# Convolution rounds with one head at full width, and another order of their horizontal distances

## The chip, the cores and the metric

The kernel runs on one core of a Trainium2 chip. The metric is the device time of one execution in microseconds (us), lower being better. A core has a matrix engine (TensorE, "PE" in the profile, its weight loads "PEld"), a vector engine (DVE), a scalar engine (ACT), GpSimd (POOL) and a sync engine (SP) that issues most of the transfers. Each engine works through its own queue in the order in which the program was written, and waits on semaphores.

## The reference, cut to what matters

Two layers work on 4 images of 512 channels, 64 x 64 pixels, all in fp32. The change is in the first layer, a linear attention with two sets of heads. The second set is made from a 5 x 5 convolution, channel by channel, of queries, keys and values, followed by a mix of 8 channels within each head:

```python
qkv = jnp.moveaxis(jnp.concatenate([q, k, v], axis=-1), -1, 1)
dw = lax.conv_general_dilated(qkv, dw_kernel, (1, 1), 'SAME', feature_group_count=3 * INNER, dimension_numbers=DN)
pw = lax.conv_general_dilated(dw, pw_kernel, (1, 1), 'VALID', feature_group_count=3 * NUM_HEADS, dimension_numbers=DN)
qkv_all = jnp.concatenate([qkv, pw], axis=1)
...
scores = jnp.einsum('bhdn,bhen->bhde', value_pad, key_)
out = jnp.einsum('bhde,bhen->bhdn', scores, query)
out = out[:, :, :-1] / (out[:, :, -1:] + EPS)
...
y = lax.conv_general_dilated(out, proj_kernel, (1, 1), 'VALID', dimension_numbers=DN)
```

'SAME' means that pixels outside the image count as zero. The second layer takes edge maps of the result, multiplies them with four weight matrices, applies gelu, weighs channels, fuses them and normalizes.

## The kernel before

**Tiling.** The 512 channels are cut into 4 groups of 128 (16 heads of 8 channels), so there are 16 pairs of image and group, each a `Group` object. An image is cut into 8 strips of 512 pixels: strip j holds every fourth row of one half of the image (`STRIPS`, L48). `project` (L256) multiplies a strip with the key or query weights of the group, four matmuls of 128 x 128 by 128 x 512 accumulated in one bank of PSUM. ACT copies the bank to an SBUF tile `s` (L268), for queries also a rectified copy (L273), and issues four DMAs (L277) that lay the strip out again for the convolution: head set n of four goes to `inps[t][:, n]`, with partitions that hold rows modulo 4 and channels, and `NB` = 17 blocks of 4 rows by `W` = 64 columns in the free dimension. One such DMA moves 64 KB to 32 partitions, for each of them 8 blocks of 64 contiguous numbers. The first and the last block of `inps` are zeros, put there once by GpSimd (L142, L143), for the rows above and below the image.

**The convolution.** `convolve` (L388) does one half of the image, for keys or queries, with matrices that hold the products of both convolutions for 4 rows and 8 channels at a time. The matrix engine is used as sixteen pieces of 32 x 32: quarter i of the partitions by head j. The result has 8 blocks of rows by 64 columns, 512 pixels, for each of 16 pieces, in four banks (`quad_tiles`, L110). Ten rounds are accumulated: five horizontal distances dx (`DXS`, L53) times two blocks b of input rows. Each round issues sixteen matmuls, j outside and i inside, so that the first is i = j = 0. A distance other than 0 reaches over the edge of the image, where the input would be zero. So the columns c0 to c1 that are read and added to are shortened (`_span`, L78): 64 columns for dx = 0 (512 pixels), 63 for 1 and -1 (504 pixels), 62 for 2 and -2 (496 pixels). The first two rounds, dx = 0, write all 512 pixels. There are 64 convolutions in the kernel: 4 images x 4 groups x keys and queries x 2 halves. ACT then takes the banks out with a rectification (L409, L415).

**Order of the work.** The order on the matrix engine is the order of the program text. Lists written out by hand in `keys_and_values` (L557) and `queries` (L587) say in which order projections (`project`, `values`), transposes (`turn`, `conv_turn`), score products (`scores`, `correlate`) and convolutions of a group follow; the keys' convolutions come in the group's own `queries`, the queries' ones in the next group's `keys_and_values`. From the second image on, the stages of the image before (`project_out`, `edge_branches`, `fuse_out`) are woven in: each listed step has an estimated time (T_CONV is 10.6), and `advance` (L881) lets as many pieces of the other stages follow as are due. The last image's stages come at the end.

**DMA queues.** SP issues loads, the values' stores for the correlation (L297, 66 KB in runs of 264 bytes) and most others. ACT's queue issues the four DMAs of a projection and the edge branches' stores (L742)[...].

Of the kernel before, what the change touches and what calls it, by code (L numbers as in the profile page):

```python
# [8 lines left out]
F32 = mybir.dt.float32  # L9
# [4 lines left out]
B, C, H, W = 4, 512, 64, 64  # L14
N = H * W
P = 128
# [30 lines left out]
NB = H // 4 + 1  # L47
# [2 lines left out]

KV_ORDER = (1, 0, 2, 3, 4, 5, 6, 7)
Q_ORDER = (6, 7, 5, 4, 3, 2, 1, 0)
DXS = (0, -2, -1, 1, 2)  # L53
VROW = 4 * 66


# [21 lines left out]
def _span(d, n):  # L78

    return max(0, -d), n - max(0, d)  # L80
# [3 lines left out]
def conv_seq_kernel(  # L84
    ctx: ExitStack, tc, x, wqkv, dpk, wtab, proj, projc, pwk, bn0, consts, vec, watt1, batt1, watt2, wbr, wfuse, out
):
    nc = tc.nc
# [7 lines left out]
    keep = front.enter_context(tc.tile_pool(name="keep", bufs=1))  # L95
# [7 lines left out]
    def work_tile(name, n=512):  # L103
        return work.tile([P, 512], F32, tag="w", name=name)[:, :n]

    def ps_tile(name):
        return psum.tile([P, 512], F32, tag="ps", name=name)

    def quad_tiles(name):
        return [psum.tile([P, 512], F32, tag="quad", name=name) for _ in range(4)]  # L110

    def squares(ap):

        return ap.rearrange("p (b x n) -> p n x b", b=4, n=4)

    def rows(ap, width=W):
        return ap.rearrange("p (r c) -> p r c", c=width)
# [20 lines left out]

    inps = {}
    for t in (KEY, QUERY):  # L140
        inps[t] = keep.tile([P, 4, NB, W], F32, name=f"inp{t}")
        nc.gpsimd.memset(inps[t][:, :, 0, :], 0.0)  # L142
        nc.gpsimd.memset(inps[t][:, :, NB - 1, :], 0.0)  # L143

    vts = []
    for n in range(3):
# [73 lines left out]
    class Group:  # L220
# [35 lines left out]
        def project(self, t, j):  # L256
            half, k = STRIPS[j]
            if (self.b, j) not in xs:
                self.load_x(j)
            ps = ps_tile("proj")  # L260
            for c in range(NCH):
                nc.tensor.matmul(  # L262
                    ps, lhsT=self.w[t][:, c, :], rhs=xs[self.b, j][c], start=(c == 0), stop=(c == NCH - 1)
                )
            if t == QUERY and (self.g == NG - 1 or self.b and j not in KV_ORDER[:2]):
                del xs[self.b, j]
            s = work_tile("strip")
            nc.scalar.copy(s, ps)  # L268

            r, b = (k + 2) % 4, 8 * half + (k + 2) // 4  # L270
            if t == QUERY:
                self.rq[j] = work_tile("rq")
                nc.scalar.activation(self.rq[j], ps, AF.Relu)  # L273
            else:
                self.strip[j] = s
            for n in range(4):
                nc.scalar.dma_start(out=inps[t][r::4, n, b : b + 8, :], in_=rows(s)[32 * n : 32 * n + 32, :, :])  # L277

        def values(self, j):
            half, k = STRIPS[j]  # L280
# [106 lines left out]

        def convolve(self, t, half):  # L388
            banks = quad_tiles("cv")
            last = len(DXS) * 2 - 1  # L390
            for n, (dx, b) in enumerate((dx, b) for dx in DXS for b in range(2)):
                c0, c1 = _span(dx, W)
                for j in range(4):
                    for i in range(4):
                        q = slice(32 * i, 32 * i + 32)
                        nc.tensor.matmul(  # L396
                            rows(banks[i])[32 * j : 32 * j + 32, :, c0:c1],
                            lhsT=self.mat[t][q, j, (dx + 2) * 8 + 4 * b : (dx + 2) * 8 + 4 * b + 4, :],
                            rhs=inps[t][q, j, 8 * half + b : 8 * half + b + 8, c0 + dx : c1 + dx],
                            start=(n == 0), stop=(n == last),  # L400
                        )
            outs = []
            for i in range(4):
                o = work_tile("co")
                if t == KEY:
                    if half == 0 and i == 0:
                        self.ksum = mini.tile([P, 4, 4], F32, name="ksum")
                    for a in range(2):
                        nc.scalar.activation(  # L409
                            o.rearrange("p (n a x b) -> p a n x b", n=4, a=2, b=4)[:, a],  # L410
                            squares(banks[i][:, 256 * a : 256 * a + 256]), AF.Relu,
                            accum_out=self.ksum[:, 2 * half + a, i : i + 1],
                        )
                else:
                    nc.scalar.activation(o, banks[i], AF.Relu)  # L415
                outs.append(o)
            self.conv[t] = outs
# [494 lines left out]
    for n, cur in enumerate(groups):  # L912
# [5 lines left out]
        if n and n % NG == 0:  # L918
            last = groups[n - 1]
# [8 lines left out]
    last = groups[-1]  # L928
# [123 lines left out]
```

## Time and profile before

| | |
|---|---|
| median of 3 runs | 5082.15 us (5077.47 to 5088.09) |
| the profiled execution | 5063.71 us, with a span of 5061.9 us |
| PE busy | 4702.0 us, 93% |
| DVE, ACT, POOL busy | 2124.7, 1626.5, 392.7 us |
| projections of keys and queries, L262 | 955.8 us of PE in 2048 records |
| output projection, L655 | 899.6 us in 2048 records |
| convolution, L396 | 730.2 us in 20480 records |
| edge branches, L730 | 495.0 us in 2048 records |
| DMA bytes | 866.26 MB, 171 GB/s in the mean |
| granted clock of PE | 0.967 |

In the profile a line of a group names the source line, the engine, the operation, what is written and read, the shape and the count; after the bar stand busy time in us, the mean length of one in ns, and the idle time of the engine just before, with what ended it. Lengths of matmuls are modelled ends of pipelined work and overlap, above all for the sixteen pieces that run side by side, so their sum is not a time. A line of the timeline has the start in us, the length of the merged stretch in us, the engine and the count. A line of the waits has the waiting engine and line, what it waited for, and the total in us, the number of times and the longest. A line of a source has the operation, the count, and the shortest, median and longest length in ns. "issue" marks idle time in which an engine waited for nothing that the profile shows.

### The profile page before, as it was taken

Reading aid. Unit: us, or ns where it says so; the run is one execution under the profiler, and the core shown is the slowest. Engines: PE = TensorE matmul, PEld = TensorE weight load, DVE = VectorE, ACT = ScalarE, POOL = GpSimd, SP = SyncE. Lnnn points to the kernel's source line nnn. Section 1 sums busy time; section 2 is a strip of 40 time slices with the busy share of each in tenths; the row PEclk is TensorE's granted clock in tenths of the full one; section 3 lists DMA queues with packets and bytes.
Section 4 is the critical chain, followed back from the end, with each engine's and each line's share of the span. In section 5 each row is a group of like instructions: output and inputs, shape, how many; then the busy total and the mean of one; then the engine's idle time right before and its main releaser. Section 6 shows DMA issues by size and latency. Waiting matters only on the chain. (4 is left out here: it accounts for less than half of the span.)

```text
span 5061.9 us, 107134 instructions
## 1 busy us (share of the span) xinstructions
PE 4702.0 (93%) x46362; PEld 2739.7 (54%) x46362; DVE 2124.7 (42%) x2960; ACT 1626.5 (32%) x2833; POOL 392.7 (8%) x291
## 2 busy tenths in 40 slices
PE   9999999999999999799899999899989898898777
PEld 5665654455666554454465655454456665445443
DVE  1222221116556433211455653431146557157965
ACT  2112111004444423200345442320024445035765
POOL 0000000000000013100000000310000000001335
PEclk9999999999999999899999999999999999999889
DMA  6444466666656565676555665657655553774425
GB/s 196 138 123 130 132 206 190 158 165 181 192 189 183 179 205 170 197 178 156 176 176 181 193 202 176 213 188 167 163 173 175 184 169 129 200 184 118 151 88 172
DMA packets 635945, 866.26 MB, mean 171 GB/s; under 512 B 324393, under 2 KB 395081, under 8 KB 617041
## 3 DMA queue, kind: packets, MB, share of 16 engines
q1 hardware_dynamic: 551504, 758.68, 51.8%
q10 hardware_dynamic: 83968, 100.74, 6.4%
q8 instruction: 364, 5.96, 0.5%
q14 instruction: 109, 0.88, 0.1%
HBM read 578.09 MB, written 213.98 MB: 156 GB/s over the span
## 5 line engine op out<-in xcount | busy, mean ns | idle before, releaser
L262 PE MATMUL proj<-xt,w_sb 128*128 128x512 f32 x2048 | 955.8, 610 | 52.9 <-DMA xt<-in_x 31.8
L655 PE MATMUL yps<-hd,fold_sb 128*128 128x512 f32 x2048 | 899.6, 596 | 9.7 <-DMA hd<-heads 8.7
L396 PE MATMUL cv<-inp,mat 32*32 32x512 f32 x20480 | 730.2, 597 | 35.4 <-issue 27.3
L262 PEld LDWEIGHTS proj<-xt,w_sb 128*128 128x128 f32 x2048 | 382.7, 194 | 523.3 <-issue 450.7
L655 PEld LDWEIGHTS yps<-hd,fold_sb 128*128 128x128 f32 x2048 | 384.9, 190 | 493.5 <-issue 445.3
L396 PEld LDWEIGHTS cv<-inp,mat 32*32 32x32 f32 x20480 | 420.3, 103 | 314.6 <-issue 154.2
L730 PE MATMUL br<-maps,wbr_sb 128*128 128x256 f32 x2048 | 495.0, 396 | 51.8 <-ACT maps L713 42.2
L808 PE MATMUL zps<-ef,wf_sb 128*128 128x512 f32 x1024 | 469.9, 610 | 53.5 <-DMA ef<-ef 19.0
L730 PEld LDWEIGHTS br<-maps,wbr_sb 128*128 128x128 f32 x2048 | 399.7, 198 | 165.9 <-issue 51.3
L284 PEld LDWEIGHTS val<-w_sb,xt 128*128 128x128 f32 x4096 | 470.2, 192 | 33.9 <-issue 26.1
L284 PE MATMUL val<-w_sb,xt 128*128 128x128 f32 x4096 | 484.9, 277 | 0.6 <-DVE vt L291 0.3
L660 DVE SCALAR_TENSOR_TENSOR yt<-yps,shift,xr 128x512 f32<-128x512 f32 x128 | 96.1, 750 | 871.8 <-PE yps L655 788.9
L268 ACT COPY strip<-proj 128x512 f32<-128x512 f32 x256 | 149.1, 582 | 928.5 <-PE proj L262 910.4
L451 PE MATMUL corr<-near,ckt 128*32 128x160 f32 x8192 | 333.6, 315 | 35.0 <-DMA near<-near 28.4
L808 PEld LDWEIGHTS zps<-ef,wf_sb 128*128 128x128 f32 x1024 | 196.1, 195 | 296.6 <-issue 235.6
L241 POOL TENSOR_TENSOR mat<-dp_sb 128x1280 f32<-128x1280 f32 x32 | 77.2, 2414 | 3464.5 <-PE cv L396 2951.0
L451 PEld LDWEIGHTS corr<-near,ckt 128*32 128x32 f32 x8192 | 256.9, 111 | 131.5 <-issue 73.1
L703 DVE TENSOR_TENSOR maps<-dv 128x1054 f32<-128x1054 f32 x128 | 162.6, 1271 | 366.9 <-PE br L730 366.9
L312 ACT ACTIVATE kt<-tr 128x512 f32<-128x512 f32 x128 | 75.8, 593 | 528.9 <-PE tr L310 345.9
L737 ACT ACTIVATE ef_o<-br,shift,scale 128x256 f32<-128x256 f32 x256 | 142.3, 559 | 283.5 <-PE br L730 251.9
L360 DVE RECIPROCAL rec<-rec 128x512 f32<-128x512 f32 x64 | 214.4, 3350 | 1.7
L812 DVE TENSOR_SCALAR z<-zps,fbias 128x512 f32<-128x512 f32 x128 | 94.9, 744 | 283.4 <-DMA out<-z 97.0
(125 smaller groups left out, 4135.7 us busy)
## 6 DMA issues: line engine op xcount, KB each, us to landing
xt<-in_x SPq DMA_DIRECT2D x316, 512.0 KB
near<-near SPq DMA_DIRECT2D x512, 264.0 KB
inp<-strip ACTq DMA_DIRECT2D x1024, 64.0 KB
win<-y SPq DMA_DIRECT2D x128, 396.0 KB
near<-vt SPq DMA_DIRECT2D x512, 66.0 KB
y<-yt SPq DMA_DIRECT2D x128, 264.0 KB
yr<-y SPq DMA_DIRECT2D x128, 264.0 KB
heads<-q SPq DMA_DIRECT2D x128, 256.0 KB
```

What stands on the lines that cost most here:

```text
L262: nc.tensor.matmul(ps, lhsT=self.w[t][:, c, :], rhs=xs[self.b, j][c], start=(c == 0), stop=(c == NCH - 1))
L268: nc.scalar.copy(s, ps)
L284: nc.tensor.matmul(ps[:, ts(c, P)], lhsT=xs[self.b, j][n][:, ts(c, P)], rhs=self.w[VALUE][:, n, :], start=(n == 0), stop=(n == NCH - 1),)
L360: nc.vector.reciprocal(rec, rec)
L396: nc.tensor.matmul(rows(banks[i])[32 * j : 32 * j + 32, :, c0:c1], lhsT=self.mat[t][q, j, (dx + 2) * 8 + 4 * b : (dx + 2) * 8 + 4 * b + 4, :],
L451: nc.tensor.matmul(self.banks[jj][32 * i : 32 * i + 32, 160 * b : 160 * b + 160], lhsT=self.held["c", i][:, at : at + 32], rhs=v[:, 4 * n ...
L655: nc.tensor.matmul(ps, lhsT=fold_sb[g // NG][:, g % NG, ts(c, P)], rhs=hd[g], start=(g == 0), stop=(g == 2 * NG - 1),)
L660: nc.vector.scalar_tensor_tensor(yt[:, :, 1 : W + 1], rows(ps), shift0[:, c : c + 1], rows(xr), ALU.add, ALU.add)
L703: nc.vector.tensor_sub(flat[:, half : 3 * half - 2], dvs[:, 2 : 2 * half], dvs[:, 0 : 2 * half - 2])
L730: nc.tensor.matmul(rows(ps)[:, 4 * n : 4 * n + 4, :], lhsT=wbr_sb[:, k, c, :], rhs=rows(maps[c // 2][:, slot[k], c % 2, :], WB)[:, :, 0:W] ...
L737: nc.scalar.activation(o[:, n, :], ps[:, 256 * n : 256 * n + 256], AF.Gelu, bias=shift1[:, k : k + 1], scale=scale1[:, k : k + 1], accum_o ...
L808: nc.tensor.matmul(ps, lhsT=wf_sb[:, k, ts(c, P)], rhs=ef[k], start=(k == 0), stop=(k == 3))
```

## The change

The head set n = 0 (j = 0 in `convolve`) gets an SBUF tile of its own, with 68 columns: two zeros on each side of the 64. GpSimd clears the whole tile once. The other three keep their layout in a tile of three. In each round the first matmul, i = j = 0, reads all 64 columns from its tile, shifted by the distance, and adds to all 512 pixels; the zeros of the border stand for the pixels outside the image. The other fifteen matmuls keep their shortened spans; those of j = 0 with i = 1, 2, 3 read the bordered tile with a shortened span. The DMA for n = 0 writes rows of 64 numbers 68 apart, 256 bytes each. The rounds are now ordered by block first: (0, 0), then b = 0 with distances -2, -1, 2, 1, then b = 1 with the same, then (0, 1) at the end. Before it was 0, 0, -2, -2, -1, -1, 1, 1, 2, 2 in distances.

```diff
-DXS = (0, -2, -1, 1, 2)
+BORDER = 2
+ROUNDS = [(0, 0)] + [(dx, b) for b in range(2) for dx in (-2, -1, 2, 1)] + [(0, 1)]
...
-        inps[t] = keep.tile([P, 4, NB, W], F32, name=f"inp{t}")
-        nc.gpsimd.memset(inps[t][:, :, 0, :], 0.0)
-        nc.gpsimd.memset(inps[t][:, :, NB - 1, :], 0.0)
+        bordered = keep.tile([P, NB, W + 2 * BORDER], F32, name=f"inb{t}")
+        nc.gpsimd.memset(bordered, 0.0)
+        inp = keep.tile([P, 3, NB, W], F32, name=f"inp{t}")
+        nc.gpsimd.memset(inp[:, :, 0, :], 0.0)
+        nc.gpsimd.memset(inp[:, :, NB - 1, :], 0.0)
+        inps[t] = [(bordered, BORDER)] + [(inp[:, j], 0) for j in range(3)]
...
             for n in range(4):
-                nc.scalar.dma_start(out=inps[t][r::4, n, b : b + 8, :], in_=rows(s)[32 * n : 32 * n + 32, :, :])
+                inp, at = inps[t][n]
+                nc.scalar.dma_start(out=inp[r::4, b : b + 8, at : at + W], in_=rows(s)[32 * n : 32 * n + 32, :, :])
...
-            last = len(DXS) * 2 - 1
-            for n, (dx, b) in enumerate((dx, b) for dx in DXS for b in range(2)):
-                c0, c1 = _span(dx, W)
+            for n, (dx, b) in enumerate(ROUNDS):
                 for j in range(4):
+                    inp, at = inps[t][j]
                     for i in range(4):
                         q = slice(32 * i, 32 * i + 32)
+                        c0, c1 = (0, W) if i == j == 0 else _span(dx, W)
                         nc.tensor.matmul(
                             rows(banks[i])[32 * j : 32 * j + 32, :, c0:c1],
                             lhsT=self.mat[t][q, j, (dx + 2) * 8 + 4 * b : (dx + 2) * 8 + 4 * b + 4, :],
-                            rhs=inps[t][q, j, 8 * half + b : 8 * half + b + 8, c0 + dx : c1 + dx],
-                            start=(n == 0), stop=(n == last),
+                            rhs=inp[q, 8 * half + b : 8 * half + b + 8, at + c0 + dx : at + c1 + dx],
+                            start=(n == 0), stop=(n == len(ROUNDS) - 1),
                         )
```

## The prediction

> **What bounds the kernel now.** I read the busy shares first, then the groups of TensorE (PE), then the waits, then single convolutions in the timeline. The page gives PE 93% of the span, far ahead of every other engine:
>
> ```profile
> PE 4702.0 (93%) x46362; PEld 2739.7 (54%) x46362; DVE 2124.7 (42%) x2960; ACT 1626.5 (32%) x2833; POOL 392.7 (8%) x291
> ```
>
> So a change counts only if it shortens PE's own stream or makes PE wait. The convolution is three groups when shapes are kept apart, 906 us in sum of which 730 us are distinct time on the page, since they overlap:
>
> ```profile
> L396 PE MATMUL cv<-inp,mat 32*32 32x496 f32 x8192 | 382.9, 588 | 7.5 <-issue 7.4
> L396 PE MATMUL cv<-inp,mat 32*32 32x504 f32 x8192 | 348.9, 595 | 20.2 <-issue 19.9
> L396 PE MATMUL cv<-inp,mat 32*32 32x512 f32 x4096 | 174.7, 618 | 7.6 <-DVE weighed L469 4.9 <-DVE cq L552 2.8
> ```
>
> Each fp32 matmul of the program is two records, two passes (20480 = 64 convolutions x 160 x 2). The 588 ns of one says nothing of the pace, as sixteen run side by side. The pace is read from the weight loads of one convolution that nothing disturbs, here the third (timeline of PEld alone, start and length in us):
>
> ```profile
> 193.25 0.23 PEld L396 LDWEIGHTS cv<-inp,mat 32*32 32x32 f32 x32 [0.17 <-issue]
> 193.70 0.10 PEld L396 LDWEIGHTS cv<-inp,mat 32*32 32x32 f32 x1 [0.22 <-issue]
> 194.13 0.55 PEld L396 LDWEIGHTS cv<-inp,mat 32*32 32x32 f32 x32 [0.32 <-issue]
> 194.99 8.02 PEld L396 LDWEIGHTS cv<-inp,mat 32*32 32x32 f32 x255 [0.30 <-issue]
> ```
>
> Rounds 0 and 1 (512 pixels) take 0.88 and 0.86 us, the eight narrower ones about 1.03 us each. It looks as if narrow rounds were the slow ones. The starts of single instructions say otherwise. Call the sixteen 32x32 pieces of the array, one for each (head j, quarter i), tiles 0 to 15 in issue order; tile 0 is i = j = 0. In this convolution:
> - A pass of 512 pixels holds its tile 429 ns, of 504 422, of 496 416, so two passes 858, 844 and 832.
> - Tiles are fed in order. A tile that is free gets its load and starts, and the next tile's load follows 16.7 ns later (6.7 ns in the first round).
> - But the next tile's load also comes no earlier than 190 ns after the tile just fed finished its previous round, and its stream can start 26.5 ns after that load: 216.5 ns from tile to tile.
>
> The rule in small windows: after tile 0 of round 1 starts at 194.13 its successor's load comes 0.19 later, and then 31 loads run through:
>
> ```profile
> 194.13 0.10 PEld L396 LDWEIGHTS cv<-inp,mat 32*32 32x32 f32 x1 [0.32 <-issue]
> ...
> 194.32 0.37 PEld L396 LDWEIGHTS cv<-inp,mat 32*32 32x32 f32 x31
> ```
>
> The decisive case is in round 4. Tile 0's previous passes ended with one from 196.24 to 196.655; its new load came at 196.66, when the tile was already free, and still the load of tile 1 waited until 196.84, again 0.19 after 196.655:
>
> ```profile
> 196.84 0.10 PEld L396 LDWEIGHTS cv<-inp,mat 32*32 32x32 f32 x1
> ```
>
> In round 5 tile 0 had been free for 160 ns, and tile 1's load waited for the remaining 30. So the 190 ns are owed whether or not a tile was free when its turn came. Applied from the first start on, these three rules give the 320 starts of this convolution within 6 ns for most and 21 ns for the worst.
>
> **What the Trainium skill says.** "TensorE: Matmul & The Clock Gate", Back-to-back issue gap, prices a pass at columns / 2.4 + 2.5 ns; with two sweeps in a record (my reading) 512 columns give 2 x 512 / 2.4 + 2.5 = 429 ns, which the trace shows. The same page, Part 3, says matmuls of different tiles start some 4 ns apart and that weight loads overlap running matmuls only in another row group. The trace has 6.7 ns in the first round, 16.7 later, and a stall of 190 ns that the page does not describe, so I use the trace. "TensorEngine Tiling (Array Packing)", Key Properties, calls the tiles independent; here they are, except for the order of feeding. "DMA: Bandwidth & Descriptors", Specifications, wants at least 512 B a piece; in the trace a 264 B packet takes 21 ns on average and ACT's 2048 B packets 103, so 1.6 times the time for a byte: it agrees in kind.
>
> **The change, part by part.**
>
> *Wide first head (tile 0 at 512 in rounds 1 to 8).* Its stream grows from 832 or 844 to 858 ns a round. A round is 1030, so tile 0 alone cannot be the bound. What is the bound? Follow the last start back through the rules: tile 1 of round 1 waits 216.5 ns after tile 0 ended round 0; tile 2 of round 2 waits 216.5 ns after tile 1 ended round 1; and so on to tile 9 of round 9. The chain steps one head on in every round. Its sum: 26 ns for the first load, 9 x 216.5 = 1949, and ten rounds of two passes, whose widths add up to 2 x 512 + 4 x 504 + 4 x 496 = 5024 pixels: 2 x 5024 x 2 / 2.4 + 20 x 2.5 = 8423. That is 10398 ns; tiles 10 to 15 follow at 16.7, +100 = 10.50 us; and the next matmul of the trace comes 0.08 later, 10.58, which the undisturbed convolutions show (10.58 in 19 of the 64). Tile 0 is on that chain only in round 0, where it had 512 already. That it now reads 8 rows of 64 out of 68 costs nothing either: the 62-of-64 reads of today take the time of their pixels, 416 ns. Cost and gain: 0.00 us.
>
> *Another order of distances.* The chain takes one round of each width, so it has the same ten terms before (512, 512, 4 narrow, ...) as after (512, eight narrow, 512). Sum again 10398 + 100. Working the rules through all sixteen tiles gives an equal end for both orders and a last start 13 ns earlier. 0.00 us, at most 64 x 0.013 = 0.8 us of gain.
>
> *The disturbed convolutions.* All 64 take 764.5 us from first start to the next matmul, 87 us over 64 x 10.58. That is instruction supply ("issue", up to 3.6 us) and waits for banks in round 0. Instruction counts are the same, so it stays. Where waits for banks spread the first round (up to 5 us), I started the rules from those starts: over all 64 the two orders end within 13 ns of each other, 0.2 ns apart in the mean.
>
> *One of four row DMAs of a projection lands in 256 B pieces.* 256 DMAs go from 32 runs of 2048 B to 256 runs of 256 B. Engine time: 65536 x 21 ns - 8192 x 103 ns = 0.53 ms over 16 engines = 33 us an engine beside DMA shares of 0.52 to 0.61: nothing waits for it. Issue on ACT's queue: the nearest row is the store of the values, 66 KB in 256 runs:
>
> ```profile
> L277 ACTq DMA_DIRECT2D inp<-strip x1024: 477/605/2537, 14.6 to 4228.5; - x171
> L297 SPq DMA_DIRECT2D near<-vt x512: 574/614/1917, 33.7 to 4141.0; - x171
> ```
>
> The piece that changes is the first of each burst of four, 477 ns today; 614 gives +0.14. Lower bound 0 (a gain has no source: no run gets longer). What stands behind it on ACT are the copies that free PE's banks: "ctr", "proj", "den" and "cden" wait for ACT some 48 times, 75 us in all.
>
> ```profile
> PE den L366 <- ACT rq L273: 26.9, 20, 7.5
> ...
> PE ctr L423 <- ACT ckt L425: 17.0, 11, 4.8
> PE proj L262 <- ACT ckt L425: 10.7, 8, 3.3
> PE cden L543 <- ACT co L415: 10.4, 4, 5.0
> ```
>
> If all were behind such a burst, 48 x 0.14 = 6.7 us; most of a burst lies beside a projection of 3.6 us, so I take 1 us. Without that cover it is the 6.7.
>
> *Zeroing.* GpSimd clears 1156 elements twice instead of border rows; at the 0.88 ns an element of its 2112-element memset that is about 1.1 us each, 1.5 us more in all. Its next work starts at 34.1 us after 28.6 us idle: hidden. What stands behind it before that is the zeros for the near borders, and the first store there is at 33.7 us. Uncovered it would be 1.5 us, once.
>
> *Waits.* The first head is its own tile now, so PE may wait on two DMA sets at a convolution's start; the strips were sent tens of us earlier. One extra semaphore instruction costs 51 ns at PE, 64 x 0.05 = 3 us if all came and all showed; I take 0.
>
> Sum against the profiled execution: 5063.7 (span 5061.9 + 1.8 around) + 0 + 1 = 5064.7. The median of the runs lies 18.4 us higher, 5082.15, so **5083 us**.
>
> **Rivals.** *Drain paid only when a tile is late.* If the 190 ns fell only on tiles still streaming at their turn, a wide first head would cover the others. The same sum under that rule gives 10.15 for 10.49 us, 0.34 x 64 = 22 us: 5060. If every round then ran at tile 0's 858 ns, the end would be 1.44 us earlier: 92 us, 4990. For it: rounds 0 and 1 do run at 0.86 to 0.88. Against it: the loads at round 4 and 5, which waited behind tiles that were free.
>
> *Short runs hold up ACT.* Some issues of this burst take 1.40 us now. If 256 runs made the changed one so, +0.92 on each burst, in 48 waits: 44 us, 5127. It decides once a burst outlasts the matmuls beside it. Against it: the 256-run store issues in 0.61.
>
> *Nothing of either, but moved addresses and DMA pieces shift the fetching of instructions*, which already varies from 0 to 3.6 us a convolution: 10 to 15 us either way.
>
> **How the numbers follow.** About 0.2% (10 us) is what can be told from no change. Forecast as worked: 0.65 same. Cheaper drain 0.15 (two thirds at 5060, one third at 4990), shifted fetching 0.05 faster and 0.06 slower, ACT 0.09. So faster 0.20, same 0.65, slower 0.15. The range leaves out 4990 and 5127: 5056 to 5104. The likeliest case alone spans 5073 to 5093.
>
> **What would show it.** Right: undisturbed convolutions still 10.58 us, last loads of a round still 1.03 us apart from round 4 on, with rounds 1 to 3 at 0.86; ACT's first issue of a burst at 0.48 to 0.62. Wrong: rounds at 0.86 to the end, or undisturbed convolutions of 9 to 10.2 us (the first rival); an ACT issue above 1 us with longer waits at "ctr" and "den" (the second).

## The result, and the profile after

| | before | after |
|---|---|---|
| median of 20 runs each | 5081.01 us (5072.85 to 5088.09) | 5071.38 us (5055.95 to 5082.98) |
| the profiled execution | 5063.71 us | 5061.49 us, span 5059.7 us |
| PE's waits by releaser: ACT, DVE, DMA | 125.8, 82.8, 87.9 us | 130.6, 94.7, 71.7 us |

After over before is 0.998, with a 95% interval of 0.9973 to 0.9988: about 10 us less, where the sum said 1 us more. The profiled execution of before happened to be a quick one, so the two spans differ by only 2 us; the ten show between the medians, and most of what made them stands, below, in one place of the trace. First the page of after:

```profile
PE 4695.3 (93%) x46362; PEld 2749.3 (54%) x46362; DVE 2126.9 (42%) x2960; ACT 1626.9 (32%) x2833; POOL 395.3 (8%) x293
...
q10 hardware_dynamic: 141312, 100.74, 7.0%
...
L816 PE MATMUL zps<-ef,wf_sb 128*128 128x512 f32 x1024 | 464.3, 604 | 30.9 <-DVE z L820 14.1
```

The busy shares hardly move. Queue 10, which ACT feeds, went from 83968 to 141312 packets and from 6.4% to 7.0%: the 57344 more packets that the short runs mean (65536 for 8192). The third line belongs to the fusing matmuls, which the diff does not touch. Set it against the line of the same group in the page of before:

```profile
L808 PE MATMUL zps<-ef,wf_sb 128*128 128x512 f32 x1024 | 469.9, 610 | 53.5 <-DMA ef<-ef 19.0
```

Its idle time fell from 53.5 to 30.9 us, and the releaser of 19.0 us, a load of `ef`, is gone. The waits of before hold it as a single event (total, times, longest):

```profile
PE zps L808 <- DMA ef<-ef: 19.0, 1, 19.0
```

Where is it? The timeline of before has it near 3272 us, here first PE (start, length, count, idle time before):

```profile
3269.50 2.84 PE L808 MATMUL zps<-ef,wf_sb 128*128 128x512 f32 x6
3291.37 2.07 PE L808 MATMUL zps<-ef,wf_sb 128*128 128x512 f32 x2 [19.03 <-DMA ef<-ef]
```

Six of the eight records of `fuse(0)` run; the last two need the fourth tile of `ef`, and PE stands still for it. The same stretch on SP's queue:

```profile
3237.31 0.33 SPq L842 DMA_DIRECT2D ef<-ef  x1
...
3242.13 1.29 SPq L842 DMA_DIRECT2D ef<-ef  x2
...
3273.55 6.36 SPq L436 DMA_DIRECT2D near<-near  x9
3279.95 0.44 SPq L842 DMA_DIRECT2D ef<-ef  x1
```

Three of the four loads were issued about 30 us ahead of need. The fourth was issued at 3279.95, and PE went on at 3291.4. Between the third and the fourth SP has 16 `near` loads of the correlation (the nine shown are the last of them) and six stores of results, and of these 37 us it stood 13.4 for the stores' data, which GpSimd makes (the waits of SP from 3242 to 3280 us):

```profile
SPq L834 <- POOL z L833: 13.4, 6, 6.5
```

A load in this place is late by all that the queue ahead of it waits for. In the kernel after the same four loads of `ef` (second image of the stage, strip 6) are issued as two and two, all ahead of the `near` loads and of those stores' waits:

```profile
3252.61 1.18 SPq L850 DMA_DIRECT2D ef<-ef  x2
...
3257.44 1.19 SPq L850 DMA_DIRECT2D ef<-ef  x2
...
3288.78 6.36 SPq L444 DMA_DIRECT2D near<-near  x9
```

and PE runs all eight records in one piece:

```profile
3284.78 3.70 PE L816 MATMUL zps<-ef,wf_sb 128*128 128x512 f32 x8
```

The wait also costs PE its full clock. The windows of before (stretch, then busy time of PE, PEld, DVE, ACT and POOL, then the granted clock) show half the clock from 3275 to 3296, so that the two records that follow took 2.07 us instead of the 0.9 that eight in 3.70 give:

```profile
3275.00:3296.00 21.00, 4.63 (x51) 1.59 (x67) 0.75 (x1) 0.69 (x1) 0.00 (x0) 0.52 0.62 204
```

In the stretch of after that holds the same work the clock is whole:

```profile
3285.00:3306.00 21.00, 21.00 (x344) 11.25 (x344) 5.24 (x10) 6.38 (x20) 6.50 (x5) 1.00 0.67 219
```

So the place costs 19.0 + 2.07 - 0.92 = 20.2 us up to the next convolution. That is the jump between the traces: measured from the start of the span, the convolution that starts at 3171.9 us in before comes 15.3 us later in after, and the one that starts at 3293.4 us comes 5.0 us earlier, 20.3 us gained between two neighbours. Apart from this, after runs late.

Why did a load move that nobody edited? Put side by side, the two kernels' instructions stand in the same order on PE, apart from the edited matmuls. On SP 18 of 2829 issues have another place (loads of weights, inputs, edge rows, `ef`), on DVE there are some 60 small exchanges, and ACT has some too. A second execution of the changed kernel (c1_after, below) has exactly the order of the first, which speaks against an order made while the kernel runs. The kernel says as much in L101, `tc.manual_schedule(engines={mybir.EngineType.PE})`: only PE's queue is held to the written order, and the others are ordered when the program is built. The description of the kernel above says of every engine that it works through its queue as the program was written; that is right for PE only, and the prediction inherits the error.

### The profile page after: what moved, and what is told of

The parts are those of the page before. It is cut to its first block, busy times and chain, and to the rows that moved or that the text cites. A ratio compares the mean times of both kernels' runs of the same rounds, so it can differ in the third digit from the quotient of the medians.

```text
span 5059.7 us, 107128 instructions
## 1 busy us (share of the span) xinstructions
PE 4695.3 (93%) x46362; PEld 2749.3 (54%) x46362; DVE 2126.9 (42%) x2960; ACT 1626.9 (32%) x2833; POOL 395.3 (8%) x293
## 3 DMA queue, kind: packets, MB, share of 16 engines
q10 hardware_dynamic: 141312, 100.74, 7.0%
## 5 line engine op out<-in xcount | busy, mean ns | idle before, releaser
L404 PE MATMUL cv<-inp,mat 32*32 32x512 f32 (+2 forms) x15360 | 709.4, 595 | 26.6 <-issue 26.3
L404 PE MATMUL cv<-inb,mat 32*32 32x512 f32 (+2 forms) x5120 | 661.2, 600 | 14.7 <-issue 6.7
L816 PE MATMUL zps<-ef,wf_sb 128*128 128x512 f32 x1024 | 464.3, 604 | 30.9 <-DVE z L820 14.1
L404 PEld LDWEIGHTS cv<-inp,mat 32*32 32x32 f32 x15360 | 306.8, 103 | 135.8 <-issue 66.6
L404 PEld LDWEIGHTS cv<-inb,mat 32*32 32x32 f32 x5120 | 225.3, 103 | 169.6 <-issue 84.8
```

The source lines that it names most:

```text
L404: nc.tensor.matmul(rows(banks[i])[32 * j : 32 * j + 32, :, c0:c1], lhsT=self.mat[t][q, j, (dx + 2) * 8 + 4 * b : (dx + 2) * 8 + 4 * b + 4, :],
L816: nc.tensor.matmul(ps, lhsT=wf_sb[:, k, ts(c, P)], rhs=ef[k], start=(k == 0), stop=(k == 3))
```

## The experiments

Five timed rounds each; the ratio is to the kernel before on the same chip, with its 95% interval.

| kernel | what it is | median, us | ratio | wait for `ef` |
|---|---|---|---|---|
| c1_after | the change | 5065.97 (before 5078.97) | 0.9969 (0.9957 to 0.998) | none |
| c1_order | new order of distances alone | 5078.87 | 1.0001 (0.9993 to 1.0009) | 19.2 us |
| c1_layout | bordered tile alone | 5063.01 | 0.9965 (0.9952 to 0.9977) | none |
| c1_wide | bordered tile and wide first head, old order | 5069.61 | 0.998 (0.9971 to 0.9988) | none |
| c2_early | before, the four loads of `ef` for one strip written a step earlier | 5058.14 (before 5078.88) | 0.9959 (0.9945 to 0.9973) | none |
| c2_late | bordered tile, the one load held back | 5087.32 | 1.0024 (1.0007 to 1.004) | 19.9 us |
| c2_early_all | before, all loads of `ef` a step earlier | 5063.02 | 0.9965 (0.9953 to 0.9976) | none |
| c2_layout_early_all | bordered tile, the same | 5069.33 | 0.998 (0.9969 to 0.999) | none |
| c3_split | own tile without a border | 5067.9 (before 5070.45) | 0.9998 (0.999 to 1.0007) | 18.5 us |

### Which part of the change carries it

Three theories were set against each other: O, the order of the distances; L, the bordered tile and what its DMAs bring with them; W, the wide first head. The change itself ran beside its parts.

> The changed kernel as it is, as the yardstick for the parts on the same chip. All theories: about 0.998 of the kernel before (5071 for 5081 us), undisturbed convolutions at 10.61 us.

> Only the new order of the rounds, on the old layout, no wide head. Theory O (the gain comes from the order): 0.998. Theory L (it comes from the layout with its short DMA runs) and theory W (it comes from the wide head): 1.000. My sum of the prediction: undisturbed convolutions end at 10.58 us as before.

```diff
-DXS = (0, -2, -1, 1, 2)
+ROUNDS = [(0, 0)] + [(dx, b) for b in range(2) for dx in (-2, -1, 2, 1)] + [(0, 1)]
...
-            for n, (dx, b) in enumerate((dx, b) for dx in DXS for b in range(2)):
+            for n, (dx, b) in enumerate(ROUNDS):
```

> Only the bordered tile with its own DMAs of 256 B runs; the first head keeps shortened spans, and the order is the old one. Theory L: 0.998. Theories O and W: 1.000 or up to 1.001, since the convolution reads rows 68 apart, which costs up to 0.035 us each (2 us in all).

```diff
-ROUNDS = [(0, 0)] + [(dx, b) for b in range(2) for dx in (-2, -1, 2, 1)] + [(0, 1)]
+ROUNDS = [(dx, b) for dx in (0, -2, -1, 1, 2) for b in range(2)]
...
-                        c0, c1 = (0, W) if i == j == 0 else _span(dx, W)
+                        c0, c1 = _span(dx, W)
```

(The first of these is an edit to before, this one and the next are edits to after.)

> The bordered tile and the wide first head, in the old order. Theory W: 0.998, with the layout alone at 1.000. Theory L: 0.998 with the layout alone at 0.998. Theory O: 1.000 or 1.001.

```diff
-ROUNDS = [(0, 0)] + [(dx, b) for b in range(2) for dx in (-2, -1, 2, 1)] + [(0, 1)]
+ROUNDS = [(dx, b) for dx in (0, -2, -1, 1, 2) for b in range(2)]
```

The order alone gives 1.0001: O falls. The bordered tile alone gives all of the gain, and the wide head on top of it gives none (0.998 after 0.9965): W falls. So the gain comes with the layout, though no instruction of the layout got shorter. Theory L had 0.998 for the layout alone, and 0.9965 lies below it by an interval that leaves 0.998 out; but the changed kernel itself came out at 0.998 on one chip and at 0.9969 on another, so a difference of 0.1% between ratios of two chips says nothing here. The traces agree with L: with the order alone SP, DVE and ACT have the order of before, instruction for instruction, and the three kernels with the bordered tile share another one. The traces also named the candidate: the kernel with the order alone still has the wait,

```profile
PE zps L808 <- DMA ef<-ef: 19.2, 1, 19.2
```

and in all three kernels with the bordered tile the waits of PE have no line for `ef` at all.

### Whether that load is the cause

Theory Q: the gain is the one load's place in SP's queue. Theory D: the bordered tile acts directly, and the load is a bystander. The load can be moved either way without touching the convolution.

> The kernel before, with the four loads of ef for strip 6 of the second image written one step earlier, so that the fourth stands ahead of the near loads in SP's queue; nothing else moves but one near and one yr load there and one product on the vector engine. Theory Q (the gain is one load's place in SP's queue): the wait of 19 us at L808 is gone, 0.9965 (5061 to 5063 for 5079). Theory D (the gain comes from the short DMA runs, the addresses or the tile split): 1.000.

```diff
+            def load_ef(j):
+                ef = []
+                for k in range(4):
+                    t = pool.tile([P, 512], F32, name="ef", tag="ef", bufs=8)
+                    nc.sync.dma_start(out=t, in_=efs[j][:, k, :])
+                    ef.append(t)
+                return ef
...
+                    ef = ahead or load_ef(j)
+                    ahead = None
...
                 if held:
+                    if b == 1 and j == 5:
+                        ahead = load_ef(j + 1)
                     norm(j - 1, *held)
```

0.9959: the kernel before with four loads written a step earlier, and nothing of the change, gains as much as the change or more (on another chip). On SP's queue all four now stand ahead of the `near` loads (the timeline again):

```profile
3244.21 0.33 SPq L840 DMA_DIRECT2D ef<-ef  x1
...
3248.87 0.87 SPq L840 DMA_DIRECT2D ef<-ef  x2
...
3254.73 0.38 SPq L840 DMA_DIRECT2D ef<-ef  x1
```

The groups of eight records of the fusing matmuls at 3264.18 and 3270.28 us run through in 3.70 us each. Only the loads of strip 6 of the second image are moved; with the fourth, one `near` load, one `yr` load and one product on DVE have another place.

> The bordered tile alone (narrow first head, old order), with the fourth load of ef for strip 6 of the second image held back behind the near loads that the program issues before it, as the kernel before has it. Theory Q: the wait of about 19 us is back, 1.000 (5079). Theory D: 0.9965 as for the bordered tile alone (5063).

```diff
-                        nc.sync.dma_start(
+                        last_near[0] = nc.sync.dma_start(
...
-                        nc.sync.dma_start(out=t, in_=efs[j][:, k, :])
+                        got = nc.sync.dma_start(out=t, in_=efs[j][:, k, :])
+                        if (b, j, k) == (1, 6, 3):
+                            tc.add_manual_dep(got.ins, last_near[0].ins.name, ...)
```

The edit fixes the place in the queue alone, it adds no semaphore. Against the bordered tile alone only this load and one store have another place on SP, and one instruction on DVE. With the load behind the `near` loads the wait is back:

```profile
PE zps L817 <- DMA ef<-ef: 19.9, 1, 19.9
```

and the gain is gone: 1.0024 where 0.9965 stood. The two convolutions named above, one on each side of the place, tell it in every trace. Their distance is 17.3 to 20.6 us shorter than in before in the seven kernels without the wait, with the border or without, and 0.1 to 1.1 us longer in the three that have it (c1_order, c2_late, c3_split below). So D falls as the source of the gain and Q holds, shown in both directions. The run missed its number all the same: with Q alone it should have come out at 1.000. It lies above that by an interval that leaves out 1, so the bordered tile costs something of its own. Two more runs ask the same with all `ef` loads early in both layouts.

> The kernel before, with the ef loads of every strip written one step earlier. Theory Q: at most as good as the single move, 0.9955 to 0.9965, as no other wait on ef over 1 us stands in the profile. Theory D: 1.000.

```diff
-                    if b == 1 and j == 5:
+                    if j + 1 < NJ:
                         ahead = load_ef(j + 1)
```

> The bordered tile alone, with the ef loads of every strip written one step earlier. Theory Q: no gain over the bordered tile alone, 0.9965, since its 19 us wait is gone already. Theory D: the two gains add up if an early load is worth anything at all; else 0.9965.

With the old layout 0.9965, with the bordered one 0.998: again the bordered tile is the slower, by 0.15%, though the two intervals touch (0.9976 and 0.9969). The second run missed theory Q's 0.9965 on the same side as the run with the load held back. Loading all strips early is no better than loading one (0.9965 and 0.9959 overlap): only one load was late.

### What moved the load

Theory S: it is the separate tile, one allocation more, that gives another built order. The alternative: the border itself, with its DMA of 256-byte rows and its larger clearing.

> The first head in a tile of its own, but without the border: rows 64 apart, DMAs in runs of 2 KB as before, old order, narrow spans. In its program the fourth load of ef for strip 6 of the second image stands behind the near loads, as in the kernel before. Theory Q: the wait of 19 us at L808 stays, 1.000 (5079), and undisturbed convolutions are at 10.58 us. Theory S (the separate tile and its own waits bring something besides the load): below 0.999.

```diff
-BORDER = 2
+BORDER = 0
```

With a tile of its own but no border, so that the rows stay contiguous, the order of SP, DVE and ACT is the old one and so is the wait (an answer of the waits):

```profile
PE zps L816 <- DMA ef<-ef: 18.5, 1, 18.5
```

with a ratio of 0.9998. S falls; the border is what shifts the build. The clearing of the whole tile was in this run too (1088 elements in 1009 ns, for 1156 in 1067 ns with the border), so by itself it moved nothing. What is left is the pitch of 68 with its DMA in runs of 256 bytes, the four columns more of the tile, or the 58 ns; these were not tried apart.

### What the bordered tile costs itself

Three comparisons at equal place of the load give +0.24% (c2_late against before), +0.15% (the two with all loads early) and +0.06% (c1_layout against c2_early, on different chips): 3 to 12 us, some 7 in the mean. Only the first is clear of noise. Two parts of that are in the traces. Convolutions with rows 68 apart take 10.60 to 10.62 us for 10.57 to 10.58, 64 x 0.02 to 0.035 = 1.3 to 2.2 us (0.02 with the pitch alone, in c1_layout, and 0.035 with the wide head and the new order too). And PE's waits at "over", nearly all for the reciprocals of the denominators, are 25.0 to 27.6 us in all six kernels with the border and 19.4 to 20.8 us in the five without: 6 us, at nearly the same places in each trace. The largest differences are moved instructions again, this time on DVE. In before, at 4177 us (timeline of DVE):

```profile
4177.20 0.70 DVE L706 SCALAR_TENSOR_TENSOR maps<-win,maps 128x524 f32<-128x524 f32 x1
4177.81 0.68 DVE L359 TENSOR_SCALAR rec<-den 128x512 f32<-128x512 f32 x1
4178.42 0.69 DVE L707 TENSOR_TENSOR maps<-maps,dv 128x524 f32<-128x524 f32 x1
4179.03 3.35 DVE L360 RECIPROCAL rec<-rec 128x512 f32<-128x512 f32 x1
```

In c1_layout the same spot has three more instructions of the edge maps ahead of the reciprocal:

```profile
4172.31 0.70 DVE L714 SCALAR_TENSOR_TENSOR maps<-win,maps 128x524 f32<-128x524 f32 x1
4172.93 0.70 DVE L726 SCALAR_TENSOR_TENSOR maps<-dv,maps 128x526 f32<-128x526 f32 x1
4173.54 0.70 DVE L715 TENSOR_TENSOR maps<-maps,dv 128x524 f32<-128x524 f32 x1
4174.16 0.70 DVE L713 TENSOR_TENSOR maps<-win 128x524 f32<-128x524 f32 x1
4174.77 0.68 DVE L367 TENSOR_SCALAR rec<-den 128x512 f32<-128x512 f32 x1
4175.37 0.70 DVE L704 TENSOR_TENSOR dv<-win 128x528 f32<-128x528 f32 x1
4175.99 3.35 DVE L368 RECIPROCAL rec<-rec 128x512 f32<-128x512 f32 x1
```

From the edge map at L706 (L714) to the reciprocal it is 1.83 us there and 3.68 us here, three times 0.62 us; PE's wait at this place went from 1.15 to 3.09 us. At five more places the wait grew, by 0.6 to 1.3 us, and there too one to three more DVE instructions stand ahead of the reciprocal; at one it fell by 0.9 us. Together that is the 6 us. The border and this order always come together in these runs, and no kernel was run that puts the instructions back, so this part is read from the traces and not shown by an experiment.

## Why the prediction was wrong, by its own steps

**Steps that held.** The rule for TensorE's tiles: the order alone leaves the undisturbed convolution at 10.57 us (10.58 before; 13 ns earlier were forecast), and the wide head adds at most 0.01 us (10.60 to 10.61 us in c1_layout and c1_wide). The stalls stand where they were forecast, in the weight loads of one undisturbed convolution of after (first head's loads alone, start and length):

```profile
196.16 0.33 PEld L404 LDWEIGHTS cv<-inb,mat 32*32 32x32 f32 x6 [0.33 <-issue]
...
197.02 0.51 PEld L404 LDWEIGHTS cv<-inb,mat 32*32 32x32 f32 x6 [0.31 <-issue]
...
199.76 0.59 PEld L404 LDWEIGHTS cv<-inb,mat 32*32 32x32 f32 x7
...
200.80 0.40 PEld L404 LDWEIGHTS cv<-inb,mat 32*32 32x32 f32 x7
```

Rounds 1 and 2 start 0.86 us apart, the later ones shown 1.04, although the first head now has 512 pixels throughout. So the first rival (a drain paid only when late, rounds at 0.86 to the end) is out. The clearing on GpSimd stayed hidden, and the DMA engines had room: 7.0% on that queue.

**Terms that were mis-sized, by little.** ACT's first issue of a burst was put at 614 ns; the source's answer of after (shortest, median and longest) has

```profile
L285 ACTq DMA_DIRECT2D inb<-strip x256: 647/648/727, 15.3 to 4223.0; - x128
```

+0.17 us, not +0.14, so above the 0.48 to 0.62 us that were to show the forecast right, and far from the 1.40 us of the second rival, which is out. PE's waits behind ACT's copies:

```profile
PE den L374 <- ACT rq L280: 29.1, 22, 7.5
PE over L383 <- DVE rec L368: 26.0, 10, 4.8
PE ctr L431 <- ACT ckt L433: 19.1, 11, 5.3
...
PE cden L551 <- ACT co L423: 12.1, 4, 5.0
PE proj L269 <- ACT ckt L433: 9.3, 7, 3.3
```

The four for ACT are 69.6 us for 65.0 in the rows shown of before, +4.6 where 1 was taken and 6.7 was the bound; the kernels without the border scatter by as much (all ACT waits of "den", "ctr", "proj" and "cden" together: 74.0 to 80.1 us without, 78.4 to 82.2 with), so the border's own part is a few us at most. Reading rows 68 apart was put at nothing, since 62 of 64 costs nothing; it costs 0.02 us a convolution by itself. And "over" was not in the sum.

**The step that failed** is the sum itself, "5063.7 ... + 0 + 1": it prices the edited instructions and takes all others to stay where they were, down to "a gain has no source: no run gets longer". It asked what each part adds to a queue and not whether the queue would keep its order. That holds for PE alone. One load of `ef` that the diff doesn't name moved ahead of 16 `near` loads and the stores between them, and with it went 20 us; moved instructions on DVE, as far as the traces tell, gave some 6 back, and with the 2 us of the convolutions the balance of 12 comes near the measured 10. That the measured time still lies within the stated 5056 to 5104 us is luck: the lower end stood for a cheaper drain, and that did not come. The third rival, moved fetching at 0.05 for the faster side, had a size and a direction like this, not the mechanism.

The material for it was at hand: the waits of before list a single 19.0 us event, and a single long wait on an unedited line can show a queue out of step with the list it serves, one exchange away from being gained or lost. Not every long wait is of this kind: one for a load of `xt`, 17.0 us in before, stands in all eleven traces (14.8 to 21.2 us). L101 says that SP's queue is free. What could not be known without building is which way the build would move it; but a case "one load of 20 us moves" belonged among the rivals with a good share of the chance.

**Left open.** Within the traces, after runs 15 us behind before until the load's place; the quick profiled execution of before accounts for part, since c2_early and c2_early_all, which have no border, are 7.0 and 11.6 us behind there too, and c2_late, with the border, is only 3.1. The rest was not followed.

## What to carry to other kernels

Before you price an edit, find out which queues keep the written order and which are ordered when the program is built: an edit elsewhere can move a load in the second kind, as the border did here and the order of distances did not, and the sum over edited instructions then has an error as large as the wait that hangs on that load. Look for such waits first (one event, many us, a DMA as releaser, an early sister load beside it) and try to remove them by writing the load earlier; here four loads written a step earlier give 5058.14 us against 5078.88, all that the change gives without its new layout. When a change moves the time, run its parts one by one before you explain it.

## What the hardware showed that was not expected

In before, the stop of 19 us brought TensorE's granted clock to half 3.4 us into the stop (at 3275.7 us, with PE idle from 3272.3), and the clock stayed there until 3296.2, 4.8 us after PE had started again; the two records behind the stop took 2.07 us for 0.92. In the stop of 17.0 us for `xt` (from 2085.4 us) the half clock came after 2.5 us and lasted until 6.0 us after the restart. A DMA of 256 runs of 256 bytes takes 648 ns to issue on ACT, where the value store of 256 runs of 264 bytes issues in 614 ns on SP.

The pitch of 68 costs time by the shift. In the undisturbed convolutions of after, in rounds 1 to 4, the wide first head's pass over eight rows of 64 takes 428 to 429 ns with a distance of 2 or -2, as without the border, and 435 to 439 ns with 1 or -1. In the first case the rows start at a multiple of four numbers (16 bytes) in the bordered tile, in the second they do not; whether that is the reason was not tried.
